# A four-layer convolution network in one kernel: the last feed-forward batch by output tiles, and part of layer 3's input formed before layer 3 begins

## The chip, the cores and the metric

The kernel runs on one core of a Trainium2 chip as one launch. Its time is device microseconds; three runs took 4709.62, 4715.95 and 4711.06 us, median 4711.06. One more execution was taken by the hardware profiler: it took 4720.24 us, with a span of 4718.5 us from the first to the last instruction. All numbers of lines (L1752 and so on) are lines of the kernel before, as the profile names them.

The core has five engines that run side by side, each in its own order: PE multiplies matrices (PEld is its loading of weights), DVE and ACT work element by element, POOL [...] issues some of the DMAs, SP only issues DMAs. Data go between HBM and the on-chip memory (SBUF) by DMA; matmuls write into PSUM.

## The reference

The input is 4 batches of 384 channels of 64 by 64 values, in float32. Four layers follow each other, each of the form x = x + f(group_norm(x)), with 32 groups:

```python
x = x + L0(gn(x))   # attention over 96 channels, 4096 positions; projection
x = x + L1(gn(x))   # 1x1 product, 8x8 block FFT filter, 3x3 depthwise conv, gated GELU, 1x1 product
x = x + L2(gn(x))   # 3x3 and 5x5 depthwise conv, batch norms, gates; feed-forward 384 -> 768 -> 384
x = x + L3(gn(x))   # per batch and channel a 7x7 kernel made from mean and maximum; depthwise conv
```

What matters here of layer 2 is its end, and of layer 3 its beginning:

```python
h1 = gelu(bn(pw(tok, cm_w1)));  h2 = bn(pw(h1, cm_w2))      # bn over all batches and positions
x2 = gate * (tok + h2) + (1 - gate) * xn + x                # xn = gn(x), the input of layer 2
# layer 3
x_avg, x_max = xn.mean((2, 3)), xn.max((2, 3))              # xn = gn(x2)
x_w = gelu(x_avg @ w_avg.T + b_avg + x_max @ w_max.T + b_max)
kern = gamma * (xr * Nx) + beta                             # xr = x_w * w_mix, Nx from its norm
out = conv7x7(xn, kern)                                     # each batch and channel its own kernel
```

A batch norm over everything stands between the product with cm_w2 and x2: no value of x2 in a channel can be formed before that channel's h2 is complete for all batches.

## The kernel before, in words

The 384 channels are three tiles j = 0, 1, 2 of 128 partitions. A batch b in one tile is 4096 values per partition; a block is a quarter of that, 1024, and is numbered i = 0 to 3 in the feed-forward, q in x2.

A framework takes the program as written, with pools of buffers, and lays out each engine's instructions in an order of its own, near the written one[...]. A buffer is given to the next tile that asks for it, and the load into it waits for the last reader of the tile before. Python generators (`next(...)` in the loops) interleave pieces of one stage with another.

**End of layer 1 (`phase_a`, `layer1`, `band_taps`, `band_out`).** The last batch has no attention beside it. Its image is taken in bands h = 0 to 7 of 8 rows. `band_taps` (L1106) makes the depthwise convolution of a band for three tiles j, partly on PE, then a GELU gate; `band_out` (L1142) makes the product, adds the input, takes statistics and stores the band (`x1`). `raw_strips` (L1160) also transposes tile 0 of each band into `z`, the large buffer of strips for layer 2's convolution, not yet normalised. The group norm is known only after band 7. `strip_factors` (L1167) and `scale_strips` (L1178) then spread its two factors over `z` and multiply and add them in: the first 32 columns on DVE, the other 96 on POOL during the first unit of `phase_b`. `matrices53` (L1387) makes the Toeplitz matrices that `conv53` (L1407) multiplies with the strips.

**Feed-forward (`phase_ef`).** The first product stores h (six tiles of 128) to HBM (`hidden`) and the sum of all else that x2 needs as `wx`. After the batch norm the second product goes through the list `jobs` (L1705): batch by batch, block by block, tile by tile. At j = 0 a block `f_h` of 3 MB is loaded (L1714) into one of two buffers and six GELUs are applied in place on ACT (L1716). `feed_back` (L1744) makes two groups of six matmuls, copies them out of PSUM on ACT and takes statistics on DVE; tile 0 stays in `z_`, the strips' memory, tiles 1 and 2 are stored as `h2`. Two jobs near the end are exchanged so that tile 0 is complete first. `h2_norms` (L1766) then gives the factor `gh` and the shift `g0` of a tile. `x2_first` (L1791) forms x2 = h2 · gh + wx for tile 0 of all four batches during the last blocks; three of them go into the three large buffers `x2_ahead` of 4096, which were filled with wx from L1722 on. `x2_piece` (L1813) takes the squares (ACT) and the maximum (DVE) of a piece; for batch 3 here, for the others later (`x2_later`, L1823).

**Layer 3 (`phase_g`).** `group_means` gives the means, `to_strips` (L2046) normalises and transposes tile 0 into `z`, and `conv7` (L2095) makes Toeplitz matrices on DVE and POOL and convolves 8 channels per call, 16 calls per tile. Beside tile 0's convolution, `x2_of` (L2024) forms x2 of tiles 1 and 2 for the four batches, eight in all: loads of wx (2 MB) and h2 (2 MB), a sum, squares, maximum, a store of 2 MB. `half_strips` (L1986) brings the next tile's strips. After tile 0, `factors` (L1924) makes the kernels' factors from all means and maxima. The raw convolution is then combined with 7 by 7 box sums in `boxes` (L2144), twelve in all, beside the convolutions of tiles 1 and 2.

Of the kernel before, what the change touches and what calls it, by code (L numbers as in the profile page):

```python
# [281 lines left out]
class _Builder:  # L282
# [223 lines left out]
    def phase_a(self, strips):  # L506
# [3 lines left out]
        with ExitStack() as ctx:  # L510
# [64 lines left out]
            layer1, done = self.layer1(B - 1), iter(())  # L575
            for n, _ in enumerate(layer1):
                if n == 20:
                    done = self.strips_of(0, range(B - 1))
                next(done, None)
            for _ in done:  # L580
                pass
# [395 lines left out]
    def layer1(self, b):  # L977
# [9 lines left out]
        for n in range(-2, 4 * 11):  # L987
# [18 lines left out]
            if alone and w == 1 and 1 < h < 10:  # L1006
                acc[h - 2] = []
                taps = self.band_taps(h - 2, alone, acc[h - 2])
            if alone and w and 1 < h < 10:
                next(taps, None)  # L1010
                yield 0.0
            if not alone and w == 1 and 1 < h < 9:
                acc[h - 2] = []
                for _ in self.band_taps(h - 2, alone, acc[h - 2]):
                    yield None if h == 8 else 0.0
# [90 lines left out]
    def band_taps(self, h, alone, acc):  # L1106
# [9 lines left out]
        for j in range(NJ):  # L1116
            acc.append(self.wk("acc", "acc", 5))
# [13 lines left out]
            if j == 2:  # L1131
                g = self.wk("gelu", "gelu", 1)
                with self.tc.high_priority():
                    first = nc.scalar.activation(g[64:P], acc[2][0:64], AF.Gelu)
                    with self.tc.issue_after(first.ins):
                        last = nc.scalar.activation(acc[0], acc[0], AF.Gelu)
                    self.ln_exp(last)
                nc.vector.tensor_mul(acc[1], acc[1], acc[0])
                nc.vector.tensor_mul(acc[2][64:P], acc[2][64:P], g[64:P])
            yield  # L1140

    def band_out(self, b, acc, h, st):  # L1142
# [11 lines left out]
        if b == B - 1:  # L1154
            self.raw_strips(b, h, x[:, 0])
        self.stats(st, x, h)
        nc.gpsimd.dma_start(self.x1[b][:, :, h * 512 : (h + 1) * 512], x)


    def raw_strips(self, b, h, x):  # L1160

        m = self.pm("strip_m")
        for k in range(4):
            self.nc.tensor.transpose(m[:, k * P : (k + 1) * P], x[:, k * P : (k + 1) * P], self.ident)
        self.nc.scalar.copy(self.z[:, :, 1 + 4 * h : 5 + 4 * h, b], m.rearrange("p (k c) -> p c k", c=P))

    def strip_factors(self, b):  # L1167

        nc = self.nc
        x = self.bx_p.tile([P, 2048], F32, tag="x", name="z_rep")  # L1170
        t, self.z_rep = (x[:, 256 * i : 256 * i + 256].rearrange("p (i c) -> p i c", i=2) for i in range(2))
        for i, v in enumerate((self.r2, self.n2)):
            nc.vector.tensor_scalar(t[:, i], self.ident, v[:, 0, b : b + 1], float(P), ALU.mult, ALU.mult)
        m = self.pm("z_rep")[:, 0 : 2 * P]
        nc.tensor.matmul(m, lhsT=self.mean128, rhs=t.rearrange("p i c -> p (i c)"), start=True, stop=True)
        nc.vector.tensor_copy(self.z_rep, m.rearrange("p (i c) -> p i c", i=2))

    def scale_strips(self, b, c0, n, eng):  # L1178

        at = slice(c0, c0 + n)  # L1180
        zv = self.z[:, at, 1:33, b]
        of = lambda i: self.z_rep[:, i, at].unsqueeze(2).to_broadcast([P, n, 32])
        eng.tensor_mul(zv, zv, of(0))
        eng.tensor_add(zv, zv, of(1))
# [15 lines left out]
    def phase_b(self):  # L1200
# [5 lines left out]
        with ExitStack() as ctx:  # L1206
# [11 lines left out]
            for n in range(LEAD + 2):  # L1218
                if n == 1:
                    self.strip_factors(B - 1)  # L1220
                    self.scale_strips(B - 1, 0, 8, nc.vector)
                if n == 3:
                    self.scale_strips(B - 1, 8, 24, nc.vector)
# [4 lines left out]
            for u in range(UNITS):  # L1228
                st = self.bt_p.tile([P, 2, 16, 6], F32, tag="st", name="st")
                tok = self.unit_tok(u - 1) if u else first  # L1230
                for n in range(16):
# [13 lines left out]
                    if not u and n in (3, 7, 11):  # L1245
                        self.scale_strips(B - 1, 8 * n + 8, 32, nc.gpsimd)
# [140 lines left out]
    def matrices53(self, n):  # L1387
# [10 lines left out]
        eng, band = (nc.gpsimd, self.band7) if n % 2 and n > 3 else (nc.vector, self.band7_p)  # L1398
# [185 lines left out]
    def phase_ef(self, strips):  # L1584
        tc, nc = self.tc, self.nc
        with ExitStack() as ctx:
# [118 lines left out]
            jobs = [(b, i, j) for b in range(B) for i in range(4) for j in range(NJ)]  # L1705
            jobs[-4:-3], jobs[-3:-2] = jobs[-3:-2], jobs[-4:-3]
            tiles, own = {}, iter(())

            for b, i, j in jobs:
                blk = slice(i * 1024, (i + 1) * 1024)  # L1710
                if j == 0:
                    h = hp.tile([P, 6, 1024], F32, tag="h", name="f_h")
                    tiles[b, i] = h
                    nc.sync.dma_start(h, self.hidden[b][:, :, blk].rearrange("o p n -> p o n"))  # L1714
                    for o in range(6):
                        last = nc.scalar.activation(  # L1716
                            h[:, o, :], h[:, o, :], AF.Gelu, bias=c1[:, o : o + 1], scale=a1[:, o : o + 1]
                        )
                    if b == B - 1 and i == 3:
                        self.ln_exp(last)  # L1720
                    if b == B - 1 and 0 < i:
                        nc.sync.dma_start(self.x2_ahead[i - 1], self.wx[i - 1][:, 0])  # L1722
                if (b, i, j) == (0, 1, 0):
                    self.mix_norms()
                for _ in range(7):
                    next(own, None)
                self.feed_back(b, i, j, w2, tiles[b, i])
                if (b, i, j) == (B - 1, 3, 0):
# [543 lines left out]
```

## Time and profile before

| | us |
|---|---|
| median of three runs | 4711.06 |
| profiled execution | 4720.24 |
| its span | 4718.5 |
| PE busy | 4359.6 (92%) |
| DVE busy | 2857.8 (61%) |
| ACT busy | 1966.8 (42%) |
| POOL busy | 813.9 (17%) |
| mean DMA rate over the span | 154 GB/s |

A busy time is that of the whole span, and the stages have different limits. The change touches four places: the passage from layer 1 to layer 2 (about 2400 to 2460), the second product of the feed-forward (3526 to 4023), the passage to layer 3 (4023 to 4065) and layer 3 itself (4065 to the end). Every float32 matmul stands as two records in the trace, so 1152 records at L1752 are 576 matmuls. In a timeline row the number after the start is the length of the group, and in brackets stand the idle time before it and what ended it.

### The profile page before, as it was taken

Reading aid. Unit: us, or ns where it says so; the run is one execution under the profiler, and the core shown is the slowest. Engines: PE = TensorE matmul, PEld = TensorE weight load, DVE = VectorE, ACT = ScalarE, POOL = GpSimd, SP = SyncE. Lnnn points to the kernel's source line nnn. Section 1 sums busy time; section 2 is a strip of 40 time slices with the busy share of each in tenths; the row PEclk is TensorE's granted clock in tenths of the full one; section 3 lists DMA queues with packets and bytes.
Section 4 is the critical chain, followed back from the end, with each engine's and each line's share of the span. In section 5 each row is a group of like instructions: output and inputs, shape, how many; then the busy total and the mean of one; then the engine's idle time right before and its main releaser. Section 6 shows DMA issues by size and latency. Waiting matters only on the chain. (4 is left out here: it accounts for less than half of the span.)

```text
span 4718.5 us, 49690 instructions
## 1 busy us (share of the span) xinstructions
PE 4359.6 (92%) x18447; PEld 2423.1 (51%) x18447; DVE 2857.8 (61%) x4675; ACT 1966.8 (42%) x2914; POOL 813.9 (17%) x758
## 2 busy tenths in 40 slices
PE   7999999999999999998978999699999999678898
PEld 2233444344443444434438888344444444578888
DVE  7766566655566455555777888655531112867788
ACT  4444444444444444443625666311123333664431
POOL 1000000000000000000026556100000000236665
PEclk9999999999999999998989999799999999888999
DMA  4311211121122112212328999866764333696887
GB/s 145 107 33 54 92 60 67 47 80 34 56 71 68 50 34 67 67 41 88 112 76 293 325 315 325 290 248 251 261 233 163 134 143 127 259 361 227 244 270 259
DMA packets 281840, 728.78 MB, mean 154 GB/s; under 512 B 22027, under 2 KB 122486, under 8 KB 269686
## 3 DMA queue, kind: packets, MB, share of 16 engines
q1 hardware_dynamic: 211336, 407.56, 27.2%
q0 software_dynamic: 38160, 172.38, 9.8%
q10 hardware_dynamic: 32094, 145.57, 7.7%
q8 instruction: 149, 2.44, 0.2%
q14 instruction: 101, 0.83, 0.1%
HBM read 431.56 MB, written 293.86 MB: 154 GB/s over the span
## 5 line engine op out<-in xcount | busy, mean ns | idle before, releaser
L819 ACT ACTIVATE probs<-sc_s 128x1024 f32<-128x1024 f32 x512 | 496.6, 1019 | 690.7 <-PE av L929 591.0
L929 PE MATMUL av<-probs,vt 128*128 128x512 f32 x1536 | 715.9, 603 | 0.0
L1128 DVE SCALAR_TENSOR_TENSOR acc<-band,vecs,acc 128x512 f32<-128x512 f32 x708 | 494.5, 745 | 49.8 <-POOL band L1089 45.3
L1752 PE MATMUL h_m<-f_h,cm_w_t 128*128 128x512 f32 x1152 | 497.2, 595 | 7.4 <-ACT f_h L1716 7.4
L1418 PE MATMUL conv_m<-toep,z 128*128 128x192 f32 (+1 forms) x2304 | 446.3, 352 | 32.8 <-DVE z L1347 12.6
L929 PEld LDWEIGHTS av<-probs,vt 128*128 128x128 f32 x1536 | 275.9, 191 | 338.6 <-issue 334.9
L1418 PEld LDWEIGHTS conv_m<-toep,z 128*128 128x128 f32 x2304 | 403.1, 195 | 56.1 <-ACT d_o L1429 14.9
L2124 PE MATMUL conv_m<-toep,z 128*128 128x128 f32 x3072 | 392.7, 286 | 39.7 <-DVE toep L2111 34.4
L2124 PEld LDWEIGHTS conv_m<-toep,z 128*128 128x128 f32 x3072 | 379.0, 202 | 41.9 <-issue 16.3
L1664 PE MATMUL h_s<-e_tok,cm_w_t 128*128 128x512 f32 x768 | 362.8, 595 | 4.1 <-DVE e_tok L1649 4.1
L1752 PEld LDWEIGHTS h_m<-f_h,cm_w_t 128*128 128x128 f32 x1152 | 219.7, 191 | 284.9 <-issue 274.1
L811 PE MATMUL sc_s<-q,k 32*128 32x512 f32 x2048 | 306.8, 643 | 14.0 <-ACT probs L819 13.9
L1399 POOL TENSOR_TENSOR toep<-w,band 128x1280 f32<-128x1280 f32 x94 | 272.5, 2899 | 184.0 <-PE conv_m L1418 184.0
L1051 PE MATMUL t_m<-w_in_t,xb 128*128 128x384 f32 x768 | 278.6, 498 | 2.8 <-DVE coef L1068 2.8
L965 PE MATMUL proj_m<-xm,w_proj_t 128*128 128x512 f32 x576 | 271.8, 611 | 6.2 <-DVE xm L904 4.9
L1671 ACT COPY e_h<-h_s 128x1024 f32<-128x1024 f32 x96 | 97.2, 1012 | 399.8 <-PE h_s L1664 399.8
L1673 DVE BATCH_NORM_STATS2 h_st<-e_h 128x6 f32<-128x512 f32 x192 | 123.5, 685 | 215.8 <-ACT e_h L1671 215.8
L1664 PEld LDWEIGHTS h_s<-e_tok,cm_w_t 128*128 128x128 f32 x768 | 146.3, 191 | 188.0 <-issue 183.3
L972 DVE SCALAR_TENSOR_TENSOR x_res<-proj_m,bn_c,x_res 128x512 f32<-128x512 f32 x96 | 71.7, 747 | 236.9 <-PE proj_m L965 236.7
L1051 PEld LDWEIGHTS t_m<-w_in_t,xb 128*128 128x128 f32 x768 | 142.6, 192 | 136.3 <-issue 54.8
L1760 DVE BATCH_NORM_STATS2 h_st<-f_h 128x6 f32<-128x512 f32 x64 | 44.2, 693 | 260.6 <-ACT f_h L1759 260.6
L1664 PE MATMUL h_s<-z,cm_w_t 128*128 128x512 f32 x384 | 196.3, 593 | 0.0
(458 smaller groups left out, 6390.4 us busy)
## 6 DMA issues: line engine op xcount, KB each, us to landing
d<-d_o ACTq DMA_DIRECT2D x48, 1024.0 KB
c_d<-d SPq DMA_DIRECT2D x48, 1024.0 KB
hid<-e_h ACTq DMA_DIRECT2D x16, 3072.0 KB
f_h<-hid SPq DMA_DIRECT2D x16, 3072.0 KB
x_in<-in_x SPq DMA_DIRECT2D x96, 256.0 KB
x_res<-in_x SPq DMA_DIRECT2D x32, 768.0 KB
xa<-x_res POOLq DMA_DIRECT2D x32, 768.0 KB, 3.9
xa_out<-xa SPq DMA_DIRECT2D x32, 768.0 KB
```

The source lines that it names most:

```text
L811: nc.tensor.matmul(s[:, g], lhsT=k4[32 * g : 32 * g + 32, c], rhs=q[i][32 * g : 32 * g + 32], start=True, stop=True,)
L819: nc.scalar.activation(p[:, h * 1024 : (h + 1) * 1024], s[:, 2 * h : 2 * h + 2].rearrange("p a b -> p (a b)"), AF.Exp, scale=0.25,)
L929: nc.tensor.matmul(av[0], lhsT=vt[:, 4 * c + v, :], rhs=p[:, v * 512 : (v + 1) * 512], start=c == 0 and v == 0, stop=c == 7 and v == 3,)
L965: nc.tensor.matmul(m, lhsT=self.w_proj[:, j, o * P : (o + 1) * P], rhs=xm[:, j], start=j == 0, stop=j == NJ - 1,)
L1051: nc.tensor.matmul(m[:, 0:C], lhsT=xb[:, j], rhs=self.w_in[:, j, :], start=j == 0, stop=j == NJ - 1,)
L1128: nc.vector.scalar_tensor_tensor(out, src(j, k), w, done, ALU.mult, ALU.add)
L1399: eng.tensor_tensor(t, self.w53[:, at : at + 160].rearrange("p (m n) -> p m n", n=8).unsqueeze(2).to_broadcast([P, 20, 8, 8]), band.rearra ...
L1418: nc.tensor.matmul(m[:, c * 256 + to : c * 256 + to + 64 * (k1 - k0)], lhsT=self.z_[:, at : at + P], rhs=t[:, 10 * c + k0 : 10 * c + k1].r ...
L1664: nc.tensor.matmul(s[:, v, :], lhsT=w1[:, j, o * P : (o + 1) * P], rhs=t[j][:, v * 512 : (v + 1) * 512], start=j == 0, stop=j == NJ - 1,)
L1673: nc.vector.bn_stats(st[:, o, 8 * b + 2 * i + v, :], h[:, o, v * 512 : (v + 1) * 512])
L1752: nc.tensor.matmul(m, lhsT=w2[:, o, j * P : (j + 1) * P], rhs=h[:, o, v * 512 : (v + 1) * 512], start=o == 0, stop=o == 5,)
L2124: nc.tensor.matmul(m[:, ch % 4 * P : (ch % 4 + 1) * P], lhsT=self.z_[:, at : at + P], rhs=t[:, 8 * c + 2 * i : 8 * c + 2 * i + 2].rearrang ...
```

## The change

Nothing of the arithmetic's result changes. In the order of the program:

1. In the last batch of layer 1, band 7's taps are written as one piece a tile slot earlier (n = 36) and in the order j = 0, 2, 1, with the product of the gate after j = 1. The raw strips and their scaling are gone. Instead tile 0 of bands 0 to 5 is loaded again from HBM in two loads (`ahead_strips`, on POOL's queue), and once the norm is known `last_strips` normalises, transposes and copies eight pieces on ACT, DVE and PE. Two of the first Toeplitz matrices of `phase_b` go to POOL.
2. In the feed-forward, batches 0 to 2 go block by block as before. The last batch goes tile by tile: all four blocks of tile 0, then of tile 1, then of tile 2. Its blocks 0 and 1 are loaded into the three large buffers at the start, its blocks 2 and 3 into the two buffers of 3 MB.
3. After tile 0 of the last batch, `x2_first` forms x2 of tile 0 for all four batches in place in `z_`, with squares and maxima at once; three are copied to the large buffers on ACT. After tile 1, `x2_second` forms x2 of tile 1 for batches 0 and 1, and stores it.
4. In layer 3, six `x2_of` are left; `factors` is cut into pieces that are interleaved with tile 0's convolution; boxes begin in tile 0 when x2 is complete; the scaling of the raw result in the boxes goes to ACT for all tiles.

```diff
-                next(done, None)
-            for _ in done:
-                pass
+                if next(done, True) is None:
+                    left -= 1
+                elif not left and len(ahead) < 2 and self.last_x1[3 * len(ahead) + 2] is not None:
+                    ahead.append(self.ahead_strips(len(ahead)))
+            self.last_strips(ahead)
...
-        for j in range(NJ):
-            acc.append(self.wk("acc", "acc", 5))
+        last = alone and h == 7
+        acc.extend([None] * NJ)
+        for j in (0, 2, 1) if last else range(NJ):
+            acc[j] = self.wk("acc", "acc", 5)
...
+    def last_strips(self, ahead):
+        nc = self.nc
+        n, r = self.n2[:, 0, B - 1 : B], self.r2[:, 0, B - 1 : B]
+        own = self.blk.tile([P, NJ, 512], F32, tag="x", name="last_x1", bufs=1)
+        pieces = [(x[:, j], x[:, j]) for x in ahead for j in range(NJ)]
+        pieces += [(own[:, i], self.last_x1[6 + i][:, 0]) for i in range(2)]
+        for i, (out, src) in enumerate(pieces):
+            if i % 4 == 3:
+                nc.vector.tensor_scalar(out, src, r, n, ALU.mult, ALU.add)
+            else:
+                nc.scalar.activation(out, src, AF.Identity, bias=n, scale=r)
+            m = (self.pa, self.pm)[i % 2]("strip_m")
+            for k in range(4):
+                nc.tensor.transpose(m[:, k * P : (k + 1) * P], out[:, k * P : (k + 1) * P], self.ident)
+            zv = self.z[:, :, 1 + 4 * i : 5 + 4 * i, B - 1]
+            mv = m.rearrange("p (k c) -> p c k", c=P)
+            if i in (1, 4, 6):
+                nc.scalar.copy(zv, mv)
+            else:
+                nc.vector.tensor_copy(zv, mv)
...
-        eng, band = (nc.gpsimd, self.band7) if n % 2 and n > 3 else (nc.vector, self.band7_p)
+        eng, band = (nc.gpsimd, self.band7) if n < 2 or n % 2 and n > 3 else (nc.vector, self.band7_p)
...
-            jobs = [(b, i, j) for b in range(B) for i in range(4) for j in range(NJ)]
-            jobs[-4:-3], jobs[-3:-2] = jobs[-3:-2], jobs[-4:-3]
-            for b, i, j in jobs:
...
+            def ready(b, i):
+                blk = slice(i * 1024, (i + 1) * 1024)
+                src = self.hidden[b][:, :, blk].rearrange("o p n -> p o n")
+                if b == B - 1 and i < 2:
+                    h, runs = [], ((0, 4), (4, 2)) if i == 0 else ((0, 2), (2, 4))
+                    for o0, n in runs:
+                        k = 6 * i + o0
+                        t = self.x2_ahead[k // 4][:, k % 4 * 1024 : (k % 4 + n) * 1024].rearrange("p (o n) -> p o n", o=n)
+                        nc.sync.dma_start(t, src[:, o0 : o0 + n])
+                        h += [t[:, o] for o in range(n)]
+                else:
+                    t = hp.tile([P, 6, 1024], F32, tag="h", name="f_h")
+                    nc.sync.dma_start(t, src)
+                    h = [t[:, o] for o in range(6)]
+                for o in range(6):
+                    self.last_gelu = nc.scalar.activation(
+                        h[o], h[o], AF.Gelu, bias=c1[:, o : o + 1], scale=a1[:, o : o + 1]
+                    )
+                tiles[b, i] = h
+            late = B - 1
+            for b in range(late):
+                for i in range(4):
+                    ready(b, i)
+                    if b == late - 1 and i > 1:
+                        ready(late, i - 2)
+                    for j in range(NJ):
+                        self.feed_back(b, i, j, w2, tiles[b, i])
+                    if (b, i) == (0, 0):
+                        self.mix_norms()
+                    if (b, i) == (late - 1, 2):
+                        ready(late, 2)
+            ready(late, 3)
+            self.ln_exp(self.last_gelu)
+            own = iter(())
+            for j in range(NJ):
+                for i in range(4):
+                    self.feed_back(late, i, j, w2, tiles[late, i])
+                    for _ in range(6):
+                        next(own, None)
+                    if j == NJ - 1 and i < 2:
+                        for b in range(1) if i == 0 else range(1, NJ):
+                            for q in range(4):
+                                at = q * 1024
+                                nc.scalar.copy(
+                                    self.x2_ahead[b][:, at : at + 1024], self.z_[:, b * N + at : b * N + at + 1024]
+                                )
+                self.h2_norms(slice(j, j + 1))
+                if j == 0:
+                    first2 = self.x2_first()
+                    own = self.in_turn(first2, self.x2_second())
+                if j == 1:
+                    for _ in first2:
+                        pass
...
     def x2_first(self):
+        for b in range(B):
+            for q in range(4):
+                at = q * 1024
+                x = self.z_[:, b * N + at : b * N + at + 1024]
+                w = self.spare() if q % 2 else self.io.tile([P, 1024], F32, tag="wx", name="f_wx", bufs=2)
+                nc.sync.dma_start(w, self.wx[b][:, 0, at : at + 1024])
+                nc.vector.scalar_tensor_tensor(x, x, self.gh[:, 0, b : b + 1], w, ALU.mult, ALU.add)
+                yield
+                self.x2_piece(0, b, q, x, self.ps("x2_sq").rearrange("p a b -> p (a b)"))
+                yield
+            nc.gpsimd.dma_start(self.scratch["x2"][b][0], self.z_[:, b * N : b * N + N])
+
+    def x2_second(self):
+        for b in range(2):
+            for q in range(4):
+                sl = slice(q * 1024, q * 1024 + 1024)
+                x = self.io.tile([P, 1024], F32, tag="wx", name="f_wx", bufs=2)
+                nc.sync.dma_start(x, self.wx[b][:, 1, sl])
+                h = self.spare() if q % 2 else self.io.tile([P, 1024], F32, tag="x", name="f_h2")
+                nc.sync.dma_start(h, self.h2[b][:, 1, sl])
+                nc.vector.scalar_tensor_tensor(x, h, self.gh[:, 1, b : b + 1], x, ALU.mult, ALU.add)
+                yield
+                self.x2_piece(1, b, q, x, self.ps("x2_sq").rearrange("p a b -> p (a b)"))
+                nc.gpsimd.dma_start(self.scratch["x2"][b][1][:, sl], x)
+                yield
...
-            x2 = others(*(self.x2_of(j, b) for j in (1, 2) for b in range(B)))
+            x2 = [self.x2_of(j, b) for j, b in ((1, 2), (1, 3), (2, 0), (2, 1), (2, 2), (2, 3))]
+            x2 = self.in_turn(*x2, self.factors())
...
-                            next(later, None)
                             if j == 0 and (k < 2 or k == 2 and n % 2):
-                                next(x2, None)
+                                x2_left = next(x2, "none") != "none"
+                            if j == 0 and not x2_left:
+                                next(boxes, None)
...
-                    self.factors()
-                    self.pair_scales(2)
...
-                if j:
-                    nc.vector.scalar_tensor_tensor(xp, d, self.a_s[:, j, b : b + 1], xp, ALU.mult, ALU.add)
-                else:
-                    nc.scalar.activation(
-                        d, d, AF.Identity, bias=self.g0[:, j, b : b + 1], scale=self.a_s[:, j, b : b + 1]
-                    )
-                    nc.vector.tensor_add(xp, xp, d)
+                nc.scalar.activation(d, d, AF.Identity, bias=self.g0[:, j, b : b + 1], scale=self.a_s[:, j, b : b + 1])
+                nc.vector.tensor_add(xp, xp, d)
```

## The prediction

> **What bounds the kernel now.** I read the stretch-by-stretch busy times first, then the timelines at the three places that the change touches, then the waits of layer 3. The stretches, in us: last feed-forward product, its tail, strips of layer 3, start of tile 0's convolution, its main part, the factors, tile 1, tile 2. Columns: microseconds, busy (and count) of PE, PEld, DVE, ACT, POOL, granted clock, DMA share, GB/s.
>
> ```profile
> 3526.00:3995.00 469.00, 468.97 (x1087) 207.53 (x1088) 67.34 (x107) 163.76 (x189) 15.43 (x29) 0.99 0.40 149
> 3995.00:4024.00 29.00, 28.22 (x66) 12.16 (x64) 26.80 (x37) 8.64 (x16) 2.65 (x5) 1.00 0.64 253
> 4024.00:4065.40 41.40, 21.07 (x135) 16.58 (x135) 33.51 (x65) 27.54 (x32) 12.71 (x29) 0.84 0.42 153
> 4065.40:4100.00 34.60, 26.15 (x198) 25.69 (x199) 31.57 (x33) 26.67 (x46) 11.00 (x7) 0.80 0.68 233
> 4100.00:4260.00 160.00, 124.05 (x975) 121.59 (x973) 111.47 (x123) 98.96 (x151) 58.89 (x50) 0.87 1.00 371
> 4260.00:4285.00 25.00, 12.43 (x64) 12.09 (x65) 15.70 (x34) 10.04 (x18) 11.24 (x13) 0.67 0.85 306
> 4285.00:4525.00 240.00, 216.23 (x1785) 212.00 (x1785) 185.50 (x245) 95.32 (x146) 159.34 (x156) 0.94 0.73 223
> 4525.00:4719.00 194.00, 177.15 (x1518) 174.69 (x1516) 169.15 (x214) 43.52 (x68) 111.88 (x96) 0.97 0.81 265
> ```
>
> See three things. The feed-forward product is bound by PE (468.97 of 469) while DMA is 40% used. Tile 0 of layer 3 is bound by DMA: share 1.00 at 371 GB/s for 160 us, after a stretch in which it idled. Tiles 1 and 2 keep PE 90% busy and DVE 77 to 87%, so little is free there. The waits of 4065 to 4285 say how the DMA reaches PE: late h2 blocks hold ACT, ACT holds DVE, DVE's Toeplitz matrices behind it hold PE.
>
> ```profile
> DVE x L2039 <- ACT x_m L2038: 34.3, 15, 6.5
> PE conv_m L2124 <- DVE toep L2111: 34.4, 8, 9.5
> ```
>
> [...] three issuing engines together, 371 GB/s, share 1.00. So bytes taken out of tile 0 are worth time there, and bytes put into the feed-forward's end compete with its other transfers; the forecast goes by 371 GB/s, the trace's figure.
>
> **Part 1, the end of layer 1.** Before, the last batch's strips are made raw, and once the group norm is known two factors are spread and multiplied in.
>
> ```profile
> 2422.02 0.69 DVE L1139 TENSOR_TENSOR acc<-acc,gelu 64x512 f32<-64x512 f32 x1 [2.03 <-ACT gelu L1134]
> 2447.37 5.15 DVE L1183 TENSOR_TENSOR z<-z,z_rep 128x256 f32<-128x256 f32 x2
> 2452.37 6.24 DVE L1184 TENSOR_TENSOR z<-z,z_rep 128x256 f32<-128x256 f32 x2
> 2455.15 15.30 PE L1418 MATMUL conv_m<-toep,z 128*128 128x256 f32 x72 [8.73 <-DVE z L1184]
> ```
>
> The norm's last value is written at 2441.5; the first convolution starts at 2455.15, 13.7 us later, behind 11.4 us of DVE. After: eight pieces are normalised (6 on ACT, about 0.63; 2 on DVE, about 0.45), transposed (0.66 for four) and copied (3 on ACT, 5 on DVE, 1.08 each, L1165). ACT 7.0, DVE 6.9 plus the four small multiplications of the swap (0.69), two hand-overs of about 0.7: z is whole about 9 us after the norm. That saves 4.5. The order 0, 2, 1 lets the taps of j=1 hide the table load and Gelu behind which DVE waited 2.03: 2 more. The 17 us of POOL for scaling hid behind unit 0 and count nothing. Since the layer's DMA is 95% busy from 2600 on, part may be lost: −5 (0 to −9).
>
> **Part 2, the last batch by tiles.** Matmuls stay 576 of about 0.857, and the loads into the large buffers (6.3 MB) take the place of as many bytes of wx at the same point, so the start costs nothing. But the last batch's blocks 2 and 3 must stay through all three tiles. In the built order block 2 of the last batch takes the buffer that (2,1) frees, so block (2,3) is given the buffer of (2,2), and its load waits for (2,2)'s last matmul. Behind that load stand six Gelus, and all of PE. The lengths:
>
> ```profile
> 3543.63 0.37 SPq L1714 DMA_DIRECT2D f_h<-hid  x1
> ...
> 3554.24 3.50 ACT L1716 ACTIVATE f_h<-f_h,bn_h_c,bn_h_a 128x1024 f32<-128x1024 f32 x3 [14.49 <-DMA f_h<-hid]
> ```
>
> Load 10.6, first Gelu 1.23: PE stands 12 us. Then the first group of six matmuls goes at the Gelus' pace, as at 3526.03, where it took 7.9 instead of 5.15: 2.8 more. +15 (13 to 17). The load of block 3 of the last batch waits in the same way, but 20.6 us of blocks 0 and 1 and 10.3 of block 2 cover its 18.
>
> **Part 3, the tail.** Tiles 1 and 2 of the last batch are 8 groups of 5.15 each, 41.2 per tile. Tile 0's x2 is formed in tile 1's time. Per pair of pieces DVE has two multiply-adds, two maxima and one statistic: 2×1.20+2×1.13+0.61 = 5.3. The spare buffer's load starts after its multiply-add and takes as long as here:
>
> ```profile
> 4001.11 0.33 SPq L1803 DMA_DIRECT2D z<-wx  x1
> ...
> 4006.19 1.28 DVE L1806 SCALAR_TENSOR_TENSOR z<-z,gh 128x1024 f32<-128x1024 f32 x1 [1.50 <-DMA z<-wx]
> ```
>
> 5.05+1.2 = 6.3 a pair; 2.4 MB per pair at 371 GB/s are 6.4 also. Starting 4.5 after tile 0's last matmul (as 3992.3 to 3996.84), the eight pairs take 49, and with tile 1's norm behind them its factor is there 15 us into tile 2 instead of 4.5. ACT's copies of products stand behind the squares, but four PSUM banks keep PE going. Then half of tile 1: each wx buffer goes load, multiply-add, store, load. Before has no such round; its parts are 4.5 (two loads in flight, near 5.05), 1.3, POOL 0.7 and a store of 6.5, between the 2.9 and 7.7 shown here for h2's stores:
>
> ```profile
> DMA to landing us min/median/max: 2.9/7.7/9.2
> ```
>
> 13 us for two pieces; three rounds and both ends make 44. So the last multiply-add ends 59 us after tile 1's last matmul, 18 after PE's own end. DVE's order has tile 2's last statistics and its norm behind it, then the group means, and everything of layer 3 waits for those: strips begin about 27 after PE's end instead of 12.1 (4023.2 to 4035.34, below; part of that was its own wait for stores). +15 (5 to 28; 10 or 16 us per round make 7 and 24, and a faster or slower tile 0 moves it by some 4). The twelve copies to the large buffers (1.0 each on ACT) fit between.
>
> ```profile
> 4035.34 1.59 DVE L2076 TENSOR_SCALAR ax<-z,s_s,s_b 128x1024 f32<-128x1024 f32 x2 [0.43 <-DMA w_gate<-in_w_avg_t]
> ```
>
> **Part 4, layer 3.** Count from the strips' start (4035.3 before). Before, x2 is complete at 225 (4260), with 560 of 1536 convolution matmuls issued; the factors take 25; the rest 433. Bytes to that point are about 70 MB: eight pieces of 6.3 (wx in, h2 in, x2 out), the rest mixing weights, raw results and strips. After, six pieces (two were formed in part 3), and in the built order the factors' first matmul stands after 407 convolutions: 37.7+3.4+6.3+3.5, and a first load for the boxes, 53 MB. The buffers of wx come free as the strips are read, from about 8 on, not after the squares and maxima of tile 0 (4065 to 4090). At 371 GB/s: 8+143, x2 complete at about 150. PE needs 103 of the 120 us after the strips (407 of 0.227, as 72 at 4065.37 took 16.36, and 66 transposes of 0.16), so DMA still sets it. The factors in pieces have 37 convolutions between their steps: 8 us of waiting are left of 25. Then 43 convolutions without boxes (11), and the rest, 110 matmuls longer than before's (28): 150+8+11+461 = 630 instead of 683. −53, and taking the scale of tile 1 and 2's boxes on ACT moves only 0.08 on DVE 16 times: −55 (−35 to −75).
>
> **Sum.** −5+15+15−55 = −30. The profiled execution took 4720.2 (span 4718.5 and 1.7 around it); 4690 would answer it. It lies 9.2 above the median 4711.06, from which I go: 4681.
>
> **Rivals.** *The moved bytes cost less than thought* (stores land in 4 us, tail +5, x2 complete by 130): −60, 4651. For it: DMA has 60% free in the product. Against it: POOL's queue carries four stores of 2 MB just then. *PE becomes the bound of tile 0 and the boxes*, gain 35: −10, 4701. For it: PE is 90% busy from 4285. Against it: 57 us of idle PE between 4065 and 4285 are there to win. *Slower: the round of x2's second tile.* If load and store queue behind each other as h2's loads do at 4100 to 4260, a round takes 30 and not 13: tail 66, sum +21, 4732. It decides from 26 a round. Against it: 3.7 MB per round is below the rate. *That x2 is not formed ahead* is no case: the built order shows it.
>
> **How the numbers follow.** Forecast 0.55 (4663 to 4699), cheaper 0.12, PE bound 0.15, slower 0.18. 0.2% (9.4 us) is about what this kernel's measurement can tell. Faster: 0.53+0.12+half of 0.15 = 0.72; same 0.09; slower 0.19. The range runs from 4645, taking in most of the cheaper case, to 4724, in which the slow case begins: a round of 27.
>
> **What would show it.** One PE gap of 12 near 3864 before block (2,3), with the load behind it; the first multiply-add on wx and h2 15 us into tile 2; strips 27 after the last product; tile 0's DMA at 1.00 for some 110 us, not 160; no gap of PE over 10 at the factors; the first strip-convolution of layer 2 nine us after the norm. I am wrong if the strips wait over 45, or tile 0 ends where it did.

## The result, and the profile after

The changed kernel takes 4733.02 us (median of eight runs, 4722.14 to 4744.10). The kernel before, run beside it, takes 4717.38 (one of its eight runs took 7855.99 and is not in the ratio; without it the median is 4715.95). The ratio is 1.0035, 95% interval 1.0020 to 1.0051: slower by about 16 us, where the forecast had it 30 faster. The profiled execution took 4734.28 with a span of 4732.5, 14.0 over the span before.

The span can be cut at events that both traces have: the start of the feed-forward's second product, the first normalisation of layer 3 on DVE ("the strips' start"), and the factors' products (g_pv first, gx_m last).

| us | before | after | difference | forecast |
|---|---|---|---|---|
| start of the second product | 3526.0 | 3512.7 | −13.4 | −5 |
| from there to the strips' start | 509.3 | 542.6 | +33.3 | +30 |
| from there to the end | 683.2 | 677.2 | −6.0 | −55 |

The first and second rows are the forecast's parts 1 to 3, the third its part 4, and there the error lies (49 us; the second row adds 3 and the first takes off 8). In the table of stretches of the changed kernel (product, its end, the tail, the strips, tile 0 to the factors' first product, the factors, and the boxes in two halves; microseconds, busy and count of PE, PEld, DVE, ACT, POOL, granted clock, DMA share, GB/s):

```profile
3512.70:3993.00 480.30, 466.90 (x1078) 206.36 (x1079) 97.99 (x143) 179.45 (x217) 15.94 (x30) 0.98 0.42 158
3993.00:4032.20 39.20, 35.20 (x76) 14.67 (x74) 23.11 (x38) 22.29 (x32) 4.77 (x9) 0.91 0.88 327
4032.20:4055.30 23.10, 0.59 (x3) 0.50 (x2) 13.51 (x32) 6.06 (x14) 3.81 (x10) 0.59 0.67 232
4055.30:4088.70 33.40, 21.78 (x133) 16.59 (x133) 27.54 (x34) 28.01 (x30) 11.16 (x24) 0.88 0.78 282
4088.70:4225.40 136.70, 109.55 (x869) 107.32 (x869) 102.65 (x116) 88.50 (x137) 59.16 (x48) 0.89 0.96 345
4225.40:4242.70 17.30, 17.26 (x123) 17.08 (x124) 11.08 (x25) 6.37 (x12) 7.19 (x8) 0.80 1.00 314
4242.70:4560.00 317.30, 274.26 (x2302) 269.61 (x2301) 245.67 (x316) 123.09 (x184) 203.63 (x196) 0.94 0.70 218
4560.00:4732.50 172.50, 145.11 (x1242) 143.05 (x1241) 137.33 (x156) 40.59 (x55) 78.55 (x65) 0.96 0.69 225
```

In tile 0 the chain shown of before, ACT's late h2 before DVE and DVE's matrices before PE, is shorter (from 4055 to 4243; 34.3 and 34.4 us before):

```profile
DVE x L2079 <- ACT x_m L2078: 23.2, 11, 7.3
```

```profile
PE conv_m L2164 <- DVE toep L2151: 18.4, 5, 8.8
```

The factors now leave PE no gap (17.26 of 17.30), as foreseen. But behind them, where before PE was busy 216 of 240 and 177 of 194, it is busy 274 of 317 and 145 of 172, with DMA at 0.70. The waits say for what. The list of waits from the factors' last product to the end, first before (4285.5 to 4718.5), then after (4242.7 to 4732.5): who waited for whom, us in total, times, longest.

```profile
PE box_m L2237 <- ACT ht L2204: 33.1, 16, 4.3
ACT in_raw L2220 <- DMA in_raw<-raw: 24.8, 11, 5.1
DVE in_x L2218 <- DMA in_raw<-raw: 8.0, 3, 4.0
```

```profile
PE box_m L2272 <- ACT ht L2244: 56.9, 18, 7.8
ACT in_raw L2257 <- DMA in_raw<-raw: 78.3, 25, 10.0
DVE in_x L2258 <- ACT in_raw L2257: 15.5, 9, 6.0
```

PE waits 24 us more for `ht`, the copy that ACT makes of the transposed box sums, and ACT waits three times as long for the raw results (the convolution's results, loaded again in pieces of 1024 to be scaled and added). Before, only tile 0's pieces are scaled on ACT; tile 1's wait is the 8.0 of DVE. The longest such wait in the changed kernel's timeline:

```profile
4397.46 0.36 SPq L2252 DMA_DIRECT2D in_raw<-raw  x1
4399.59 1.95 PE L2164 MATMUL conv_m<-toep,z 128*128 128x128 f32 x16
4407.54 1.24 ACT L2257 ACTIVATE in_raw<-in_raw,g,a_s 128x1024 f32<-128x1024 f32 x1 [9.97 <-DMA in_raw<-raw]
4408.68 0.56 ACT L2244 COPY ht<-ht_m 128x512 f32<-128x512 f32 x1
4409.30 2.08 PE L2272 MATMUL box_m<-cols,ht 128*128 128x128 f32 x8 [7.76 <-ACT ht L2244]
4411.41 0.75 DVE L2274 SCALAR_TENSOR_TENSOR in_x<-box_m,b_s,in_x 128x512 f32<-128x512 f32 x1 [8.54 <-PE box_m L2272]
4412.02 3.41 PE L2164 MATMUL conv_m<-toep,z 128*128 128x128 f32 x16
```

ACT stands 9.97 us at the scale of a raw piece whose load was issued 10 us before, with a ready `ht_m` (transposed at 4399.2) behind it. PE stands 7.76 at the product that needs the copy, DVE 8.54 at the addition behind that. ACT did not take the copy while it stood: the copy began at 4408.68, behind the scale, 8.9 us after its transposes had ended (4399.76). After the wait PE runs at about half pace: 16 convolution records take 3.41, ahead of it 1.95.

### The profile page after: what moved, and what is told of

It is laid out like the page before. It is cut to its first block, busy times and chain, and to the rows that moved or that the text cites. A ratio compares the mean times of both kernels' runs of the same rounds, so it can differ in the third digit from the quotient of the medians.

```text
span 4732.5 us, 49819 instructions
## 1 busy us (share of the span) xinstructions
PE 4361.6 (92%) x18445; PEld 2422.0 (51%) x18445; DVE 2863.7 (61%) x4676; ACT 1986.9 (42%) x2929; POOL 808.6 (17%) x763
## 5 line engine op out<-in xcount | busy, mean ns | idle before, releaser
L1791 PE MATMUL h_m<-f_h,cm_w_t 128*128 128x512 f32 x1008 | 440.9, 600 | 24.8 <-ACT f_h L1728 20.8
L1791 PEld LDWEIGHTS h_m<-f_h,cm_w_t 128*128 128x128 f32 x1008 | 193.7, 193 | 271.5 <-issue 238.9
L1405 POOL TENSOR_TENSOR toep<-w,band 128x1280 f32<-128x1280 f32 x96 | 278.0, 2896 | 200.2 <-PE conv_m L1424 187.7
L837 PE MATMUL av<-probs,vt 128*32 128x512 f32 x1536 | 189.0, 604 | 4.5 <-DVE av_t L866 4.5
```

The costliest lines, as they stand in the source:

```text
L837: nc.tensor.matmul(av[k][quarter(g)], lhsT=vt[:, 4 * c + v, quarter(s)], rhs=p[:, v * 512 : (v + 1) * 512], start=c == 0 and not before, s ...
L1405: eng.tensor_tensor(t, self.w53[:, at : at + 160].rearrange("p (m n) -> p m n", n=8).unsqueeze(2).to_broadcast([P, 20, 8, 8]), band.rearra ...
L1791: nc.tensor.matmul(m, lhsT=w2[:, o, j * P : (j + 1) * P], rhs=h[o][:, v * 512 : (v + 1) * 512], start=o == 0, stop=o == 5,)
```

## The experiments

All runs are compared with the kernel before, which took 4713.0 to 4715.6 beside them. A ratio less 1, times 4715, gives the difference in us; the changed kernel stands at +16.5. It was not run again beside the experiments, and by the intervals of both ratios a difference from it is good to about 8 or 9 us.

**e1: the end of layer 1 alone.** The kernel before with the change's part 1 (`ahead_strips`, `last_strips`, the order of band 7, two matrices on POOL).

> Only the first part (end of layer 1) is put into the kernel before. The two traces show the first convolution on the strips 11.2 us earlier and the second product of the feed-forward 13.4 us earlier. If that is the part's own worth, the kernel takes about 4704 us, 13 less than the kernel before (4717); if the 13 come from chance in the passage and the part is worth what the prediction gave it, 4712; if later stages give it back, no change. In the trace the second product should begin near 3513.

4705.74, ratio 0.9978 (0.9966 to 0.9990): −10.4 us, between −16 and −5. The part holds its gain to the end, and it is about twice what the forecast gave it. (The −13.4 of the table is less sure: in e7, which is the kernel before up to layer 3, the second product begins at 3510.8 and not 3526.0, and in the profiled runs that have part 1 it begins anywhere from 3494.7 to 3512.7. The second row is steady: 509.3, 508.9 and 509.1 in the kernel before, e1 and e7, 540.7 to 542.6 in the changed kernel, e2, e3 and e5.) PE's timeline at the end of the last bands, before and then in the changed kernel:

```profile
2412.35 3.70 PE L1121 MATMUL taps_m<-band,diag 128*128 128x512 f32 x8 [0.84 <-DVE acc L1128]
2423.49 2.08 PE L1148 MATMUL out_m<-acc,w_out_t 128*128 128x512 f32 x2 [7.44 <-DVE acc L1138]
```

```profile
2404.75 3.70 PE L1130 MATMUL taps_m<-band,diag 128*128 128x512 f32 x8
2408.29 1.02 PE L1160 MATMUL out_m<-acc,w_out_t 128*128 128x512 f32 x2
2414.83 2.07 PE L1160 MATMUL out_m<-acc,w_out_t 128*128 128x512 f32 x2 [2.36 <-DVE acc L1151]
2444.00 6.17 PE L1424 MATMUL conv_m<-toep,z 128*128 128x256 f32 x19 [0.84 <-POOL toep L1405]
```

PE's wait before the last band's product falls from 7.44 to 2.36, since its last taps now run ahead of the rest of band 6's product and not behind it. From band 6's first product to the end of band 7's it is 31.8 us before (2403.8 to 2435.6) and 24.1 after. The passage from the norm to the first convolution fell from 13.7 to 11.4 only. The strips were whole at 2442.04, 9.3 after the norm as forecast; then PE still had two small products in its order and waited for a Toeplitz matrix that the change makes on POOL (2.90 us each there, 1.49 on DVE, by the medians of L1405), as the last row says. The earlier slot of the taps and their new order were not tried apart.

**e4: the other buffer.** In the changed kernel, block 2 of the last batch is made ready after block (2,3).

```diff
-                    if (b, i) == (late - 1, 2):
-                        ready(late, 2)
+            ready(late, 2)
             ready(late, 3)
```

> The changed kernel, with block 2 of the last batch made ready after block (2,3), so that (2,3) gets the buffer that (2,1) left and not that of (2,2). By the prediction's second part the gap of 13.4 us near 3868 and the slow group behind it go: 14 to 17 us faster than the changed kernel, 4716 to 4719. If the stand of the last batch's blocks 2 or 3 takes its place, 4725 to 4733, with a new gap of PE before them.

4717.74, ratio 1.0001 (0.9993 to 1.0010): 16 us faster than the changed kernel. PE's timeline there, changed kernel and e4:

```profile
3868.55 12.01 PE L1791 MATMUL h_m<-f_h,cm_w_t 128*128 128x512 f32 x23 [13.40 <-ACT f_h L1728]
```

```profile
3839.47 40.93 PE L1790 MATMUL h_m<-f_h,cm_w_t 128*128 128x512 f32 x95
```

The gap is gone and no other takes its place (from the product's start to the strips' start: 526.0 against 542.6).

**e2: the raw scale of tile 1 on DVE again.** In the boxes of the changed kernel; the shift of tile 1 is left out of the output.

```diff
-                nc.scalar.activation(d, d, AF.Identity, bias=self.g0[:, j, b : b + 1], scale=self.a_s[:, j, b : b + 1])
-                nc.vector.tensor_add(xp, xp, d)
+                if j:
+                    nc.vector.scalar_tensor_tensor(xp, d, self.a_s[:, j, b : b + 1], xp, ALU.mult, ALU.add)
+                else:
+                    ...
```

> The changed kernel, with the scale of tile 1's raw result in one multiply-add on DVE again instead of ACT and then DVE (the shift of tile 1 is left out of the output by that). Theory A: ACT waits for the raw loads in its fixed order, with the copies of the box sums behind it, and PE waits for those; 37.6 us of such waits fall in tile 2, and PE's wait for the copies is 20 us there against 8 before. Then the kernel gets 12 to 20 us faster than the changed one (4733), to 4713 to 4721, and PE's wait for the copies in all falls from 57 to about 40. Theory B: the boxes are late because they now begin in tile 0 and meet other transfers; then there is no change, 4730 to 4735.

4718.60, ratio 1.0007 (0.9998 to 1.0016): 13 us faster than the changed kernel. PE's wait for the copies fell to 45.5, ACT's wait for raw results to 39.0. Theory A holds for what tile 1's scale cost; most of PE's waits stay. The size is less sure by this run alone: in its profiled execution the stretch from the factors' last product to the end is only 5.6 shorter (484.2 against 489.8).

**e7: the same step alone, in the kernel before.** Tile 1's multiply-add on DVE becomes a scale on ACT and an addition on DVE.

> The kernel before, with tile 1's raw scale on ACT and an addition on DVE, as the changed kernel has it; nothing else. If this by itself costs what its removal gave back in the changed kernel (13 us), 4727 to 4731; PE's wait for the copies of the box sums rises from 33 to about 45. If it costs only together with boxes that begin in tile 0, 4715 to 4718.

4729.49, ratio 1.0028 (1.0017 to 1.0039): +13.2. So the step costs 13 us by itself (8 to 18), whatever the rest does. Its waits from the factors' last product to the end, which takes 450.1 and not 433.0:

```profile
PE box_m L2239 <- ACT ht L2206: 42.5, 18, 7.1
ACT in_raw L2220 <- DMA in_raw<-raw: 44.3, 14, 9.1
ACT in_raw L2222 <- DMA in_raw<-raw: 20.2, 9, 4.9
```

PE's wait for the copies was 33.1, and about 45 was expected; ACT's wait for raw results was 24.8 and is 64.5 in both lines. DVE has one pass over 1024 values either way (1.28 us before, 1.22 in e7); what changes is which queue stands when the load is late: for tile 1's pieces DVE stood 8.0 us before, ACT stands 44.3 in e7.

**e3: the raw load written three steps earlier.**

```diff
+            if j < NJ - 1:
+                d = self.gt_p.tile([P, 1024], F32, tag="rest", name="in_raw", bufs=3)
+                nc.sync.dma_start(d..., self.raw[j]...)
             yield
...
             self.box_sums(j, b, x, 2 * part + 1, ht)
             if j < NJ - 1:
-                d = self.gt_p.tile(...)
-                nc.sync.dma_start(...)
```

> The changed kernel, with the load of the raw piece written three steps earlier in the boxes (at the head of its part) and the scale on ACT left where it is. If the wait of ACT for the raw load is what holds PE (theory A), ACT's 78 us of waits fall below 30, PE's wait for the copies of the box sums from 57 to under 30, and the kernel takes 4695 to 4710. If the loads are late because the DMA engines are full (theory B), the waits only move and it takes 4728 to 4738.

4730.64 (4707.93 to 4744.77), ratio 1.0030 (1.0021 to 1.0039): no gain that can be told. Its profiled execution was the fastest of its runs, so only its waits are read. SP's queue in e3's boxes:

```profile
SPq L2239 <- DVE in_x L2259: 96.9, 17, 8.9
```

The loads stand in SP's queue for a buffer: three are shared with the convolution's results, and here one comes free mostly with an earlier addition of a raw piece. In the changed kernel this wait was 12.3, but there the loads stood for the stores of results that held the buffers (39.8 and 29.3); all waits of that load in the boxes together are 86 there and 120 in e3. ACT still waits 81.7 for raw results. Writing the load earlier doesn't load earlier here; this was a failed mend. Its time lies where theory B had it, but it doesn't decide between the theories, since the load did not come sooner.

**e5: the boxes held back until tile 1.**

```diff
-                            if j == 0 and not x2_left:
-                                next(boxes, None)
```

> The changed kernel, with the boxes held back until tile 1's convolution (as in the kernel before). Theory B: by starting in tile 0 the boxes of tile 0, with their raw loads, fall wholly into convolutions 768 to 1024, where the strips of tile 2 are loaded; that stretch takes 137.7 us in the changed kernel and 122.9 in the kernel before. If so, it returns to about 123, and from the factors' last product to the end it takes about 15 (68 convolutions without boxes) + 22 + 433 + 13 for tile 1's scale on ACT = 483 instead of 490: 4723 to 4729. If the start in tile 0 is not the cause, that stretch keeps its 137 and the boxes merely end later: 4733 to 4745.

4713.02, ratio 0.9994 (0.9983 to 1.0004): 19 us faster than the changed kernel, and faster than the expected 4723 to 4729. From the factors' last product to the end it takes 472.3 and not 489.8, and PE is busy as long (421.4 and 419.4): it is waiting that went. The stretch named in the expectation, convolutions 768 to 1024, counted by record, with its waits for the copies and the raw results, first in the changed kernel, then in e5:

```profile
4388.70:4523.10 134.40, 110.24 (x905) 108.48 (x904) 98.69 (x123) 53.94 (x80) 78.56 (x73) 0.90 0.78 243
PE box_m L2272 <- ACT ht L2244: 23.9, 6, 7.8
ACT in_raw L2257 <- DMA in_raw<-raw: 32.5, 9, 10.0
```

```profile
4361.10:4487.00 125.90, 109.72 (x904) 106.97 (x903) 94.93 (x122) 52.70 (x77) 77.27 (x74) 0.95 0.83 255
PE box_m L2270 <- ACT ht L2242: 11.6, 8, 4.1
ACT in_raw L2255 <- DMA in_raw<-raw: 10.3, 7, 3.9
```

These convolutions take 126 us again, as before the change (125.3), and not 134; the 137.7 of the expectation is a window that holds 530 convolution records where the other has 512. So this stretch answers about half of the gain. The rest is spread: from the factors to convolution 512 it is 21.9 and not 29.3, from 512 to 768 105.2 and not 116.7, and behind 1024, where the boxes held back fall, 219.3 and not 209.4.

That boxes begun in tile 0 cost 19 us is shown; why is shown in part. The DMA engines are fuller in the faster run (0.83 against 0.78), so it is not that they are full on the mean. Nor is it the number of raw pieces in the stretch (11 against 10), but their place may count: the first is scaled 4 us ahead of the stretch, in e5 46 us into it. What makes their loads late is open. For the longest wait, the load of 0.5 MB was issued at 4397.46 behind one of 2 MB at 4396.83, at which SP's queue itself had stood 16.6 us for a buffer. The next two waits (5.99 at 4440.79, 5.67 at 4479.11) come behind strip loads of 0.34 MB. None of these was tried alone.

**e8: the other buffer, boxes from tile 1, and the earlier raw load together.**

> The changed kernel with three edits: the other buffer for block (2,3), the boxes held back until tile 1, and the raw load three steps earlier. The first was worth 16; if the boxes' waits come from loads that meet the strips of tile 2, the second and third together take off 10 to 25: 4692 to 4708. If the second and third give nothing beside each other, 4716 to 4720.

4696.03, ratio 0.9952 (0.9937 to 0.9968): −22.6 us. The first two by their own runs give 16.5 − 16 − 19.3 = −18.8; the third adds nothing that stands out of the interval.

**e6: no x2 of tile 1 ahead.** `x2_second` is gone, and `x2_of` runs for all eight pieces of tiles 1 and 2.

> The changed kernel without x2 of tile 1 formed ahead: layer 3 forms eight pieces again less tile 0, that is all eight of tiles 1 and 2. By the prediction's sums the strips begin about 15 us sooner (no rounds behind the product, no gap of PE at its end) and x2 is complete 2 x 6.3 MB at 371 GB/s = 34 us later: 4748 to 4756. If these bytes are hidden in tile 0 beside the convolution, it is 4716 to 4722, and the forming ahead of tile 1 was a loss.

4717.62, ratio 0.9995 (0.9980 to 1.0010): 15 us *faster* than the changed kernel, against the sums. By its trace the strips start 23.5 sooner after the product's start (519.1 against 542.6) and the factors' first product comes 46.7 later after them (216.8 against 170.1), as the sums' sign has it; but from the factors' last product to the end it takes 452.3 and not 489.8. Its x2 is complete so late that the boxes do not begin before tile 1. So this run mixes two causes, and e10 below parts them.

**e9: all mended.** The other buffer, boxes from tile 1, tile 1's raw scale on DVE. Tile 1's shift is added in x2 as in the kernel before; in the part formed ahead, on ACT:

```diff
-                nc.vector.scalar_tensor_tensor(x, h, self.gh[:, 1, b : b + 1], x, ALU.mult, ALU.add)
+                nc.scalar.activation(h, h, AF.Identity, bias=self.g0[:, 1, b : b + 1], scale=self.gh[:, 1, b : b + 1])
+                nc.vector.tensor_add(x, x, h)
```

> The changed kernel with the three mends that the runs single out: the other buffer for block (2,3) (worth 16), the boxes held back until tile 1 (worth 20), and tile 1's raw scale in one multiply-add on DVE as in the kernel before (worth 13); so that the shift is in tile 1's x2 again, the part formed ahead adds it on ACT (8 times about 1.1 us, beside the product). If the three add up, 4684; if the second and third mend the same waits, 4694 to 4698.

4682.95 (4681.82 to 4693.43), ratio 0.9936 (0.9922 to 0.9949): −30 us against the kernel before, −47 against the changed one. The three add up: 16.5 − 16 − 19.3 − 13 = −31.8 from their own runs, as near as these can tell. No other version here is faster; the next two can't be told from it. Its waits in the boxes (its profiled execution, 4693.43, was the slowest of its five):

```profile
PE box_m L2273 <- ACT ht L2242: 29.4, 14, 4.1
ACT in_raw L2258 <- DMA in_raw<-raw: 26.5, 11, 5.9
```

**e10: all mended, no x2 of tile 1 ahead.**

> As the run with all three mends, but without x2 of tile 1 formed ahead. Traces so far: each further piece in layer 3 takes 23.4 us (216.8 against 170.1 for two), and the tail behind the product is 23.5 shorter without it. So forming it ahead should be worth 23 x 2 - 23.5 less what the later start of the boxes saves: with the boxes held back in both, I expect this run 3 to 25 us slower than the one with it; if it is equal or faster, the forming ahead of tile 1 is a loss whatever the boxes do.

4687.28, ratio 0.9943 (0.9929 to 0.9957): 0.07% above e9, inside the interval. By the traces the strips start 28.6 sooner (503.8 against 532.4), the factors' first product comes 53.7 later (221.1 against 167.4), and the rest is 20.3 shorter, since more of the convolution is done by then: 4.8 in favour of the forming ahead. So that part of the change, as e9 has it, is worth about nothing (3 us, which these runs can't tell from nothing). In e9 it carries the shift of tile 1 on ACT: from the product's start to the strips' start e9 takes 532.4, e4 526.0. Whether it would pay without that was not tried.

**e11: x2's first quarters between the strips.** In e9, `next(x2)` twice after the strips of batch 0 and of batch 1.

> As the run with all three mends, and the first four quarters of x2 in layer 3 are formed between the strips of batches 0, 1 and 2, not behind them. The prediction let the 53 MB of tile 0 begin 8 us after the strips' start; two runs together (170.1 us for six pieces, 216.8 for eight) say that the first piece begins with the strips' end at about 30. If that late start is what made x2 late, the factors' first product comes 5 to 15 us earlier after the strips' start than 170, though the first convolution is 4 to 10 later, and the kernel gains 0 to 10. If the DMA rate alone sets it, the factors come no earlier and the kernel loses 0 to 8.

4685.34, ratio 0.9942 (0.9923 to 0.9960): no different from e9. But the mechanism shows: the factors' first product comes 155.9 after the strips' start and not 167.4, the first convolution 43.6 and not 33.7. So x2 was late in good part because its work began behind the strips; what it gains is given back by the convolution.

## Why the prediction was wrong

*Part 1, −5, was too small*: −10.4 in e1. The direction was right; "The order 0, 2, 1 lets the taps of j=1 hide the table load and Gelu [...]: 2 more" was mis-sized. The bands' end gained 7.7, because the taps also came off the path behind band 6's product. The passage gained 2.3 where 4.5 were forecast: the strips were whole in time, but the first convolution was not ready to start with them. The busy DMA, to which a part was to be lost, took nothing back: its share is 0.95 to 0.97 only from 2600 to 2900 of the kernel before, and 0.59 to 0.89 from there to 3500.

*Part 2, +15, was right*: a gap of 13.40 at 3868.55 and a slow group behind it; 16 in e4.

*Part 3, +15, was right in sum, in part by luck.* The changed kernel's rounds on DVE, first and last, and PE's last group:

```profile
4004.55 1.28 DVE L1858 SCALAR_TENSOR_TENSOR f_wx<-z,gh,f_wx 128x1024 f32<-128x1024 f32 x1
...
4046.41 1.28 DVE L1858 SCALAR_TENSOR_TENSOR f_wx<-z,gh,f_wx 128x1024 f32<-128x1024 f32 x1
4055.32 1.57 DVE L2116 TENSOR_SCALAR ax<-z,s_s,s_b 128x1024 f32<-128x1024 f32 x2
4024.30 7.92 PE L1791 MATMUL h_m<-f_h,cm_w_t 128*128 128x512 f32 x12 [3.95 <-ACT f_h L1798]
```

The last multiply-add ends 15.5 behind PE's end at 4032.2 (forecast 18), the strips start 23.1 behind it (27), three rounds take 41.9 from first to last (3 × 13 = 39). But the first round begins 20.7 into tile 2 (its first matmul is at 3983.83), not 15. And "four PSUM banks keep PE going" failed: ACT's copies of products stand behind squares that wait for these rounds, so PE itself waits 3.95 and its last group takes 7.92 instead of 5.15; tile 2 takes 48.4 instead of 41.2. That PE ends later hides the later rounds. Parts 2 and 3 together: +30 forecast, +33.3 measured. The slower rival (a round of 30) fell.

*Part 4, −55, failed*: −6. Its chain, counted from the strips' start, was 150 + 8 + 11 + 461 = 630. Measured: the factors' first product at 170.1, their last 17.3 later (forecast 19), and 489.8 from there, 677.2 in all. Two steps failed.

1. "The buffers of wx come free as the strips are read, from about 8 on [...] At 371 GB/s: 8+143." The bytes were right: the stretches to the first product make 33.4 × 282 + 136.7 × 345 = 57 MB, 54 of them after the first 8 us, against 53. The rate was not: 282 GB/s while the strips are made and 244 from 4090 to 4110, and only from there about the forecast's. The loads of h2 stand in SP's queue for ACT's work on x2, which comes behind the strips:

```profile
4090.00:4110.00 20.00, 20.00 (x182) 20.00 (x181) 18.63 (x22) 15.06 (x25) 10.03 (x7) 1.00 0.83 244
4110.00:4225.40 115.40, 88.25 (x681) 86.02 (x679) 82.96 (x93) 72.13 (x110) 49.12 (x42) 0.87 0.99 362
SPq L2074 <- ACT g_h L1868: 90.9, 21, 10.3
```

Six pieces take 170.1, eight take 216.8 (e6): 23.4 a piece, so by an estimate from these two the first begins at about 30. The term is 20 us too short; e11, which starts the work sooner, takes 11.5 of that off.
2. "[...] the rest, 110 matmuls longer than before's (28): 150+8+11+461 = 630 [...], and taking the scale of tile 1 and 2's boxes on ACT moves only 0.08 on DVE 16 times". (The 16 are tile 1's alone; tile 2's boxes load no raw result.) The pace of the boxes was priced by work and not by queue. The scale on ACT costs 13 (e2, e7), since a late raw load now holds the copies of the box sums and with them PE. And boxes that begin in tile 0 were counted as free while they moved tile 0's raw loads: 19 (e5). The sum of 32, good to about 10, answers the 29 that the row is too long; in the profiled executions alone the two make 5.6 and 17.5. Had what is queued behind the moved instruction on ACT been named, as it was for block (2,3), the wait of 24.8 that the kernel before already shows there would have been the price to start from.

The sign "I am wrong if [...] tile 0 ends where it did" came: all 512 convolutions of tile 0 are issued 216.7 us after the strips' start, and were at 215.1. The factors' first product comes 62 us sooner after the strips' start (170.1, before 232.5), but that shortened the gap at the factors and not the convolution of tile 0. The rival "PE becomes the bound" does not answer it: PE is busy 109.55 of the 136.7 us before the factors, and idles 70 of the 490 behind them.

## What to carry to other kernels

A step moved to another engine is priced by the waits that it brings to that engine's queue: here 16 passes of 1.24 us on ACT, which is a third busy there (163.7 of 489.8), cost 13 us, because their input is a transfer and a copy that PE needs stands behind it. Work that is started earlier moves its loads too (boxes begun in tile 0 cost 19 us here); ask what they meet there. And when several parts of a change pull both ways, run each undone alone: here three small mends turned +16 us into −30, and one part, x2 of tile 1 formed ahead, gave nothing that could be measured.

## What the runs showed of the hardware

In the changed kernel some of PE's waits cost more than their length. After the wait of 7.76 us at 4409.30 the next 28 records at least (8 box products, 4 transposes, 16 convolutions) ran at about half pace, 2.9 us more than the same groups take a little later (1.06, 0.60 and 1.95); the granted clock was 0.53 from 4409.3 to 4415.5 and 1.00 from there to 4425. From the factors to the end PE has eight waits of 3.64 to 7.76 us, and behind all eight the next 24 records take 4.3 to 5.5 us instead of 2.9, at a granted clock of 0.50 to 0.67; of its eleven waits of 1.16 to 3.33 us, two are followed so (1.97 at 4301.39 and 2.27 at 4499.08), and behind the other nine the clock was 1.00. So the length of a wait does not tell by itself what follows it. The last band's product of layer 1 in the changed kernel ran at half pace (2.07 a pair of records, where band 6's at 2408.29 took 1.02) from its start at 2414.83 to its end 12 us later, at a granted clock of 0.50, and that after a wait of only 2.36:

```profile
2424.84 2.07 PE L1161 MATMUL out_m<-acc,w_out_t 64*128 64x512 f32 x2
```

Why it stayed slow there is open.
